# The passage between two steps of a graph layer on one core: the order of the last tiles' work

## The chip, the core and the metric

The kernel runs on one core of a Trainium2 chip. A core has five engines that run at the same time, each with a queue of its own in strict order: TensorE (PE in the profile; its weight loads are PEld), VectorE (DVE), ScalarE (ACT), GpSimd (POOL) and SyncE (SP), which here only issues DMAs. They wait for one another through semaphores. TensorE writes to PSUM; VectorE and ScalarE read it from there.

The metric is the device time of one execution in microseconds (us), lower is better. Several executions are timed; one more is profiled, and its trace gives the times of single instructions, counted from the start of the span.

## What is computed

A graph layer over N = 3327 nodes with D = 256 features, in two steps. `x` is normalised and passed through relu before (X below). Each step builds an attention matrix from the present features, keeps in each row only the largest probabilities that together reach 0.9, and multiplies; beside it the features are spread over a given sparse graph S.

```python
def _top_p_attention(X, W1, W2, W3):
    logits = (X @ W1.T @ W2.T) @ (X @ W3.T).T / TAU
    probs = softmax(logits)
    ...
    A = probs * mask          # mask: the largest that together reach TOP_P = 0.9
    return A / A.sum(-1)

R = S + I;  R = R / R.sum(-1)
Xf = Xa = X;  Z = 0
for n in range(2):
    A = _top_p_attention(Xa, W1, W2, W3)
    Xf = R @ Xf
    Xa = A @ Xa
    Z = Z + Xf @ U1[n].T + Xa @ U2[n].T
out = x + layernorm(X + Z) * ln_g + ln_b
```

## The kernel before

**Tiles and stages.** The 3327 rows are 26 tiles of 128 (NT = 26). For each step and tile these stages run:

- `weights`: the logits of a tile against all keys, in four chunks (CUT = 4). Each chunk is two matmuls into the PSUM buffer `pl` (L597) and an exponential by ScalarE into the row buffer `e` (L601, the last chunk L607 and L609). A chunk n needs the keys of its quarter of the tiles; the fourth needs the last tile's keys.
- `measured`: guesses the threshold of each row from sums over `e`. In step 1 (`measured_twice`) ScalarE passes three times over the whole row (`through`, L632), with small instructions of ScalarE, VectorE and POOL between the passes (L684, L685, L698 to L713). It needs the law of the tile (`ms`): from `law_once` for the first three tiles of step 1, from `laws` (eight groups of up to three tiles, L555 to L562) for the others.
- `settle`: VectorE finds the exact threshold: a pass over `e` (L728), maxima of segments (L733, L740), and the pass that sets the small entries to zero (L759 in two parts for the first and the last tile, L762 otherwise).
- `Sums`: TensorE transposes `e` in seven blocks of four (`turn`, L808), ScalarE copies them out (L810), TensorE multiplies with the features (`sum`, L822) into the single PSUM buffer `pa`. At the end of a tile of step 0 ScalarE scales the sum into `xa` (L831).
- `spread` (graph sum): six products of gathered neighbours into the single PSUM buffer `pr` (L928), then VectorE's reciprocal and sum (L1123, L1124), and in step 0 a store to `vx` in device memory. The neighbours of step 1 are gathered by POOL from `vx` (L920, indirect DMAs) and so need all of `vx`.
- `first_end` (step 0): the scaled sum is transposed (L477, copied at L480), multiplied with both U2 at once into `pr` (512 columns, L947), and the results are copied by ScalarE to `xw` (the features that step 1 sums) and, with `x0` added by POOL, to the store `sx`. Then `prep` makes the tile's keys and queries (L488, copied at L496 and L497), and for the tiles in COUNTED their part of the Gram matrix `gsum`.
- `moments` (L510 to L515) turns `gsum` into the matrix from which `law_once` (L528, L530, L536 to L543) and `laws` take mean and variance. `prove` checks the thresholds with some thirteen small VectorE instructions.

**The order.** All stages are Python generators. The loop over `i` from -1 to NT + 1 in each step has seven parts per round (PARTS = 7), and for each part a string names which generators take a step: `s` spread, `e` first_end, `w` logits, `m` and `n` measured, `d` and `c` settle, `l` laws, `g` gathers, and so on. After a part's letters follow the transposes and the sum of one block, tile i - 1 in step 0. The strings stand in BEGIN (first rounds of step 0), PLAN, OPEN (first rounds of step 1) and LAST. At the end of the function a dependency is added from each instruction of TensorE, ScalarE, VectorE and POOL to the next one in the text, so these queues run in the order of the text; SP's queue is tied that way only up to the start of step 1.

**Around the passage.** In step 0, round i = 25 sums tile 24, round 26 sums tile 25 but for its last block, and round 27 does that block. Each of the rounds also runs `spread` and `first_end` of tile i - 2. Three chunks of logits of tiles 0, 1 and 2 of step 1 (`begun`) run in rounds 24, 25 and 26. At the end of round 26 stand `moments` and three `law_once`. Step 1 begins with the last chunk of tile 0's logits, `prove(0)` and two memsets; its round -1 measures tile 0 with the laws' groups between, round 0 settles tile 0 and measures tile 1, and in round 1 the first sum starts.

The lines that order this before:

```python
for c in ("lcnwqsepb" if i > -1 else "cnwqsepb") if step else "ocmwqseph" + "b" * (i > 0):
    run(work[c])
if step == 0 and i == NT:
    moments(1, gsum)
    for t in range(3):
        live[1, t]["ms"] = returned(law_once(1, t))
```

Of the kernel before, what the change touches and what calls it, by code (L numbers as in the profile page):

```python
# [9 lines left out]
F32 = mybir.dt.float32  # L10
# [4 lines left out]
ALU = mybir.AluOpType  # L15
# [321 lines left out]
DIRECT = 4  # L337
LIST = 16
KT = DIRECT + 2
BEHIND = mybir.DependencyInfo(mybir.DependencyClass.Sync, mybir.DependencyReason.DATA)  # L340
IN_ORDER = mybir.DependencyInfo(mybir.DependencyClass.NoSync, mybir.DependencyReason.DATA)
NONE = NP - 1
# [3 lines left out]
def guess_graph_layer(ctx, tc, x, adj, w1t, w2t, w3t, u1t, u2t, ln_g, ln_b, out, flag):  # L346
# [122 lines left out]
        G.tensor_tensor(rstd, rstd, half[:, :1], ALU.pow)  # L469
        return rstd  # L470

    def transposed(rows, pt=None, xT=None):

        if pt is None:
            pt = ps_t.tile([P, 4, P], F32, tag="pt", name="pt")
        for c in range(ND):
            PE.transpose(pt[:, c, :], rows[:, c * P : (c + 1) * P], ident)  # L477
        if xT is None:
            xT = tpool.tile([P, ND, P], F32, tag="xT", name="xT", bufs=2)
        S.copy(xT, pt[:, :ND, :])  # L480
        return xT


    def prep(xT, t):
        j, h = divmod(t, 2)
        pk = ps_t.tile([P, 4, P], F32, tag="pt", name="pk")
        for c in range(ND):
            PE.matmul(pk[:, 0, :], wk[:, c, h * DA : h * DA + P], xT[:, c, :], start=c == 0, stop=c == ND - 1)  # L488
        if t in COUNTED:
            for c in range(ND):  # L490
                PE.matmul(pk[:, 1, :DA], xT[:, c, :], wk[:, c, :DA], start=c == 0, stop=c == ND - 1)
        kp = (low, high)[h]
        kr = krs[:, t // 2 % 2, :]
        if t in COUNTED:
            S.copy(kr[:, :DA], pk[:, 1, :DA])
        S.copy(after[kp, j, :], pk[kp, 0, :])  # L496
        S.copy(query_of(t), pk[query_at(t), 0, :])  # L497
        if t not in COUNTED:
            return
        yield  # L500
        pg = ps_t.tile([P, 4, P], F32, tag="pt", name="pg")
        PE.matmul(pg[:DA, 0, : DA + 1], kr[:, :DA], kr, start=True, stop=True)
        gt = small.tile([DA, DA + 1], F32, tag="gt", name="gt", bufs=2)
        S.copy(gt, pg[:DA, 0, : DA + 1])
        G.tensor_tensor(gsum, gsum, gt, ALU.add)
# [15 lines left out]
            nc.sync.dma_start(qT[rows], query_of(t))  # L521
        return qT

    def law_once(step, t):

        pq = ps_t.tile([P, 4, P], F32, tag="pt", name="pq")
        pm = pq[:, 1:3, :].rearrange("p a b -> p (a b)")[:, : 2 * DA + 2]
        PE.matmul(pm, query_of(t), qm[query_at(t), step, :], start=True, stop=True)  # L528
        mq = small.tile([P, 2 * DA + 2], F32, tag="mq", name="mq", bufs=2)
        S.copy(mq, pm)  # L530
        yield


        ms = small.tile([P, 9], F32, tag="ms", name="ms")
        col = lambda k: ms[:, k : k + 1]
        V.scalar_tensor_tensor(mq[:, : DA + 1], mq[:, : DA + 1], 1.0, mq[:, DA + 1 :], ALU.mult, ALU.mult,  # L536
                               accum_out=col(1))
        minus = mq[:, 2 * DA + 1 :]
        G.tensor_tensor(col(2), col(1), half[:, 1:2], ALU.pow)
        G.tensor_scalar(ms[:, 3:7], of_s[:, step, :], col(2), 1.0e-4, ALU.mult, ALU.add)  # L540
        G.tensor_scalar(col(7), col(1), 0.5, minus, ALU.mult, ALU.subtract)
        G.tensor_scalar(col(7), col(7), 0.25, LNY[step] - 0.25 * math.log(0.1 / N), ALU.mult, ALU.add)
        G.tensor_scalar(col(8), col(1), minus, col(4), ALU.subtract, ALU.add)  # L543
        return col


    def laws(ts):

        at = lambda k, a, b: law[:, k, a:b]
        few_of = [ts[h::2][n : n + 3] for n in range(0, len(ts), 3) for h in range(2)]  # L550
        for few in filter(len, few_of):
            pq = ps_t.tile([P, 4, P], F32, tag="pt", name="pq")
            pm = pq.rearrange("p a b -> p (a b)")[:, : 3 * (2 * DA + 2)].rearrange("p (t n) -> p t n", t=3)
            for k, t in enumerate(few):
                PE.matmul(pm[:, k, :], query_of(t), qm[query_at(t), 1, :], start=True, stop=True)  # L555
            wide = scan.tile([P, NP], F32, tag="w", name="wide")
            mq = wide[:, : 3 * (2 * DA + 2)].rearrange("p (t n) -> p t n", t=3)
            V.tensor_copy(mq[:, : len(few)], pm[:, : len(few)])
            V.tensor_copy(law[:, 2, few[0] : few[-1] + 1 : 2], mq[:, : len(few), DA])
            for k, t in enumerate(few):  # L560
                V.scalar_tensor_tensor(mq[:, k, : DA + 1], mq[:, k, : DA + 1], 1.0, mq[:, k, DA + 1 :],
                                       ALU.mult, ALU.mult, accum_out=at(1, t, t + 1))  # L562
            yield
        a, b = ts[0], ts[-1] + 1
        s, var, m = (at(k, a, b) for k in range(3))
        S.activation(s, var, AF.Ln, bias=con(7))
        S.activation(s, s, AF.Exp, scale=0.5)
        for k, c in ((3, SQG[1][0]), (4, SQG[1][2]), (5, -SQK[1][0]), (6, -SQK[1][2])):
            G.tensor_scalar(at(k, a, b), s, c, 1.0e-4, ALU.mult, ALU.add)
        G.tensor_tensor(at(4, a, b), at(4, a, b), var, ALU.add)  # L570
        G.tensor_tensor(at(4, a, b), at(4, a, b), m, ALU.add)
        G.tensor_scalar(m, m, 0.25, LNY[1] - 0.25 * math.log(0.1 / N), ALU.mult, ALU.add)
        G.tensor_scalar(var, var, 0.125, None, ALU.mult)
        G.tensor_tensor(var, var, m, ALU.add)
# [361 lines left out]
    def stores():  # L936
        while kept:
            t, sv = kept.popitem()
            nc.sync.dma_start(sx[t], sv)

    def first_end(t):
        aT = transposed(live.pop(("r", t)))
        stores()
        yield
        pz = ps_r.tile([P, 2 * D], F32, tag="pr", name="pz")
        for c in range(ND):
            PE.matmul(pz, aT[:, c, :], u2[:, c].rearrange("p n d -> p (n d)"), start=c == 0, stop=c == ND - 1)  # L947
        S.copy(xw[:, t, :], pz[:, D:])
        sv = row.tile([P, D], F32, tag="sv", name="sv", bufs=2)
        S.copy(sv, pz[:, :D])  # L950
        G.tensor_tensor(sv, sv, x0[:, t, :], ALU.add)
        yield
        kept[t] = sv
        yield from prep(aT, t)
# [30 lines left out]
        V.tensor_copy(flag, pf[:1, 0, :1])  # L985

    none = iter(())
    own_of, kept = {}, {}
    live, ohs, acs, xgs, done, early = {}, {}, {}, {}, [], {}

    def run(work, n=99):
# [139 lines left out]
    def refetch(t):  # L1131
# [14 lines left out]
    BEGIN = {-1: ("mba", "mmbba", "mwwbbaa", "bmwwb", "", "", ""),  # L1146
             0: ("mdbb", "mcdbb", "medbwwbp", "mdbb", "gmpdbwwb", "hgdbgbq", "hgq"),
             1: ("ggmdsssbb", "gmcdgsssbb", "gedbwwbp", "bmsdg", "gmpdeg", "hgdwwqg", "hgemgqo"),
             2: ("gmdsssa", "gmcdsssga", "gedawwpg", "gmsdga", "gmspdea", "ohgdawwqg", "gehmgq")}
    OPEN = {-1: ("llcmss", "lnms", "lwwnfd", "lcmdsssggggg", "fmgdswqdf", "llmdf", "lmwfdm"),  # L1150
            0: ("cmssggg", "nms", "wwnfd", "cmdsss", "fdsmgwqdf", "mdf", "mwd"),
            1: ("cmss", "nms", "wwnfd", "cmdsssgggg", "fdsmwqdf", "mgdf", "mwdg")}
    OPEN[2] = OPEN[3] = OPEN[1]
    spacing = itertools.chain(spaced((0, 1)), *(spaced((t,)) for t in range(2, NT)))
    fetching = itertools.chain(*(refetch(t) for t in range(NT)))
    LATE = (1, 4)
    BLOCKS = ({}, {1: (0, 1), 2: ()})
    trace, begin = nc.cur_bb.bb.instructions, len(nc.cur_bb.bb.instructions)
    work = dict(m=none, d=none, f=none)
    later = {}  # L1160
    ordered = []
    for step in range(2):
        sums = Sums(step, live, xw if step else x0, AHEAD[step])

        for i in range(-1, NT + 2):
# [3 lines left out]
                ordered.append(len(trace))  # L1169
            if step == 1 and i == -1:  # L1170
                run(begun[0])
                prove(0)
                for e in es[4:]:
                    G.memset(e[:, N:NP], 0.0)
            work.update(
                n=work["m"],
                c=work["d"],
                d=settle(step, i, live[step, i]) if valid(i) else none,
                m=measured(step, live[step, i + 1]) if valid(i + 1) else none,
                s=spread(step, i - 2 + 2 * step) if valid(i - 2 + 2 * step) else none,  # L1180
                w=later.pop((step, i + 2), none),
                e=first_end(i - 2) if step == 0 and valid(i - 2) else none,
                a=itertools.islice(lister, 6) if step == 0 else none,
# [9 lines left out]
                next(later[step, i + 3])  # L1193
            if step == 0 and i >= NT - 2 and i < NT + 1:

                work["w"] = itertools.islice(begun[i - NT + 2], CUT - 1)
            if step == 0 and i >= NT - 3 and i < NT:
                next(begun[i - NT + 3])
            if i == -1:
# [1 line left out]
            if step == 0 and i == 0:  # L1201
                work["w"] = begun[2]
            for k in range(PARTS):
                g = PARTS * (i - 1) + k - LATE[step]
                summing = valid(g // PARTS)
                if step and valid((g + AHEAD[1]) // PARTS):
# [17 lines left out]
                run(work["m"])  # L1224
            if step == 0 and i == -1:
                G.memset(es[2][:, N:NP], 0.0)
            if step and i < 1:
                next(fetching)
            for c in ("lcnwqsepb" if i > -1 else "cnwqsepb") if step else "ocmwqseph" + "b" * (i > 0):
                run(work[c])  # L1230
            if step == 0 and i == NT + 1:
                stores()
            if step == 0 and i == NT:
                moments(1, gsum)
                for t in range(3):
                    live[1, t]["ms"] = returned(law_once(1, t))
    run(work["f"])

    for engine, since, until in ((PE.engine, begin, None), (S.engine, begin, None), (V.engine, begin, None),
# [48 lines left out]
```

## Time and profile before

| what | us |
|---|---|
| three timed runs, median (lowest to highest) | 1344.52 (1342.86 to 1345.33) |
| the profiled execution, its own time | 1346.05 |
| its span, first to last instruction | 1344.3 |
| TensorE busy in the span | 1259.3 (94%) |
| VectorE busy | 1151.8 (86%) |
| ScalarE busy | 1074.2 (80%) |
| GpSimd busy | 1017.4 (76%) |

The busy shares are means over the span. Step 0 runs to about 741 us, step 1 from there. In the windows from 200 to 690 us TensorE is busy for 99.9% of the time, and between 900 and 1300 us for 95 to 97%. Between 740 and 760 us it is busy for 13.49 of 20 us, and between 760 and 800 us for 24.54 of 40. A group in the trace is named by line, engine and tile: `pa` is the sum of weighted features, `pr` the graph sum, `pz` the U2 product, `pk` the keys, `pl` logits, `pt` transposes, `pq` moments and laws. Where a row has a bracket, it gives the idle time of the engine in front of it and what ended it.

### The profile page before, as it was taken

Reading aid. Unit: us, or ns where it says so; the run is one execution under the profiler, and the core shown is the slowest. Engines: PE = TensorE matmul, PEld = TensorE weight load, DVE = VectorE, ACT = ScalarE, POOL = GpSimd, SP = SyncE. Lnnn points to the kernel's source line nnn. Section 1 sums busy time; section 2 is a strip of 40 time slices with the busy share of each in tenths; the row PEclk is TensorE's granted clock in tenths of the full one; section 3 lists DMA queues with packets and bytes.
Section 4 is the critical chain, followed back from the end, with each engine's and each line's share of the span. In section 5 each row is a group of like instructions: output and inputs, shape, how many; then the busy total and the mean of one; then the engine's idle time right before and its main releaser. Section 6 shows DMA issues by size and latency. Waiting matters only on the chain.

```text
span 1344.3 us, 22106 instructions
## 1 busy us (share of the span) xinstructions
PE 1259.3 (94%) x6396; PEld 956.0 (71%) x6396; DVE 1151.8 (86%) x3481; ACT 1074.2 (80%) x2315; POOL 1017.4 (76%) x1411
## 2 busy tenths in 40 slices
PE   5989899999999999999999589999999999999985
PEld 4535677778777787777777367777777777777774
DVE  6876899999999999999981698888998898988993
ACT  5476798888878888888853889899998999999951
POOL 6214888888888888887883587888888888888852
PEclk9999999999999999999999789999999999999998
DMA  7744455454555555455433213132222223131200
GB/s 265 254 132 133 123 153 160 141 157 136 144 157 145 154 142 155 137 152 154 117 103 91 79 50 90 54 95 62 86 79 69 87 65 95 53 95 61 82 24 23
DMA packets 100723, 153.13 MB, mean 114 GB/s; under 512 B 16849, under 2 KB 67152, under 8 KB 100592
## 3 DMA queue, kind: packets, MB, share of 16 engines
q1 hardware_dynamic: 83056, 108.72, 25.5%
q0 software_dynamic: 16640, 42.69, 12.7%
q8 instruction: 53, 0.87, 0.3%
q14 instruction: 78, 0.64, 0.2%
q10 hardware_dynamic: 896, 0.21, 0.1%
HBM read 120.88 MB, written 27.28 MB: 110 GB/s over the span
## 4 chain that ended last, share of the span: by engine, by line
PE 52%; ACT 25%; POOL 10%; DVE 7%; issue 3%; DMA 0%; SPq 0%; DVEq 0%; POOLq 0%; ACTq 0%
PE pa L822 23%; ACT ja L632 14%; PE pl L597 7%; PE pt L808 6%; PE pr L928 5%; PE pz L947 3%; PE pz L1016 3%; POOL g L710 3%; ACT eT L810 3%; ACT e L601 2%; POOL xg L920 2%; DVE cand L733 1%; ACT x L601 1%; DVE bb L740 1%; POOL g L707 1%
## 5 line engine op out<-in xcount | busy, mean ns | idle before, releaser
L822 PE MATMUL pa<-xw,eT 128*128 128x256 f32 x1352 | 323.7, 384 | 4.0 <-DVE s L958 3.8
L632 ACT ACTIVATE ja<-e,g 128x3328 uint8<-128x3328 f32 x106 | 325.7, 3073 | 0.1
L822 PE MATMUL pa<-x,eT 128*128 128x256 f32 x1352 | 322.0, 379 | 0.0
L822 PEld LDWEIGHTS pa<-xw,eT 128*128 128x128 f32 x1352 | 250.7, 190 | 64.0 <-issue 20.9
L822 PEld LDWEIGHTS pa<-x,eT 128*128 128x128 f32 x1352 | 242.8, 190 | 25.5
L733 DVE MAX8 cand<-w 128x8 f32<-128x168 f32 (+1 forms) x1040 | 253.4, 317 | 0.0
L810 ACT COPY eT<-pt 128x512 f32<-128x512 f32 (+1 forms) x364 | 198.4, 553 | 45.4 <-PE pt L808 39.1
L899 POOL DMA_INDIRECT ac<-in_adj,index x130 | 188.2, 1448 | 60.1 <-issue 26.5
L920 POOL DMA_INDIRECT xg<-bx,index x130 | 184.4, 1419 | 48.6 <-issue 16.2
L808 PE MATMUL pt<-ident,e 128*128 128x128 f32 x1144 | 176.0, 276 | 17.1 <-DVE e L759 8.5
L920 POOL DMA_INDIRECT xg<-vx,index x130 | 164.3, 1264 | 34.0 <-issue 32.9
L808 PEld LDWEIGHTS pt<-ident,e 128*128 128x128 f32 x1144 | 138.8, 143 | 71.0 <-issue 44.1
L728 DVE SCALAR_TENSOR_TENSOR w<-e,g 128x3328 f32<-128x3328 f32 x44 | 164.4, 3737 | 9.1 <-ACT g L713 8.2
L928 PE MATMUL pr<-xg,ac 128*128 128x257 f32 (+1 forms) x520 | 141.5, 396 | 10.4 <-DVE s L1124 7.0
L762 DVE SCALAR_TENSOR_TENSOR e<-e,rec 128x3328 f32<-128x3328 f32 x40 | 147.2, 3680 | 0.6
L601 ACT ACTIVATE e<-pl 128x832 f32<-128x832 f32 x132 | 113.9, 865 | 27.7 <-PE pl L597 24.5
L928 PEld LDWEIGHTS pr<-xg,ac 128*128 128x128 f32 x520 | 93.8, 194 | 37.5 <-issue 14.6
L597 PE MATMUL pl<-both,qT 64*128 64x416 f32 x416 | 100.0, 545 | 7.7 <-ACT e L601 4.3
L597 PE MATMUL pl<-after,qT 64*128 64x416 f32 x416 | 95.9, 555 | 1.8 <-ACT e L601 1.4
L852 DVE TENSOR_REDUCE fm<-at 128x4 f32<-128x512 f32 (+1 forms) x133 | 84.3, 634 | 0.0
L740 DVE MAX8 bb<-cand 128x8 f32<-128x160 f32 x234 | 75.6, 323 | 4.6
L632 ACT ACTIVATE ja<-x,g 128x3328 uint8<-128x3328 f32 x24 | 73.7, 3069 | 0.0
(261 smaller groups left out, 2045.3 us busy)
## 6 DMA issues: line engine op xcount, KB each, us to landing
at<-in_adj SPq DMA_DIRECT2D x114, 256.0 KB
cx<-ac SPq DMA_DIRECT2D x26, 384.0 KB
ac<-cx SPq DMA_DIRECT2D x26, 384.0 KB
wide<-in_adj SPq DMA_DIRECT2D x8, 832.0 KB
e<-in_adj SPq DMA_DIRECT2D x6, 832.0 KB
own<-bx SPq DMA_DIRECT2D x26, 128.5 KB
x<-in_x SPq DMA_DIRECT2D x13, 256.0 KB
qT<-both SPq DMA_DIRECT2D x104, 32.0 KB
```

Source lines behind the costliest of these rows:

```text
L597: PE.matmul(pl[:, a, :wd], qT[p, :], keys_of(step, a).rearrange("p a b -> p (a b)")[:, c : c + wd], start=True, stop=True)
L601: S.activation(e.rearrange("p (a n) -> p a n", a=2)[:, :, c : c + wd], pl[:, :, :wd], AF.Exp, accum_out=za[:, n : n + 1])
L632: S.activation(ja, e, f, bias=guess, scale=sign, accum_out=total)
L728: V.scalar_tensor_tensor(w, e, col(16), e, ALU.is_lt, ALU.mult, accum_out=d2)
L733: V.max(cand[:, 8 * s : 8 * s + 8], w[:, s * SEG : min(NP, (s + 1) * SEG)])
L762: V.scalar_tensor_tensor(e, e, at(1), e, ALU.is_ge, ALU.mult, accum_out=ra)
L808: PE.transpose(pt[:, j, :], e[:, (j0 + j) * P : (j0 + j + 1) * P], ident)
L810: S.copy(eT[:, :w, :], pt[:, :w, :])
L822: PE.matmul(self.pa, eT[:, c - 4 * k, :], self.xa[:, j, :], start=c == 0, stop=c == NT - 1)
L899: G.indirect_dma_start(out=ac[:, k, :], out_offset=None, in_=rows, in_offset=bass.IndirectOffsetOnAxis(ap=index[:, t, k : k + 1], axis=0), ...
L920: G.indirect_dma_start(out=xg[:, k, :w], out_offset=None, in_=rows, in_offset=bass.IndirectOffsetOnAxis(ap=index[:, t, k : k + 1], axis=0))
L928: PE.matmul(pr[:, :w], ac[:, k, :], own if k == KT - 1 else xg[:, k, :w], start=k == 0, stop=k == KT - 1)
```

## The change

Tiles 23, 24 and 25 (ENDS = 3) have their U2 product taken out of `first_end`: there the sum is transposed and the keys are made at once, and the transposed sum is kept in `ends`. The graph sums of tiles 24 and 25 are taken out of rounds 26 and 27. Both come back in a new generator `middle`, whose letter is `x`, in round -1 of step 1: two graph sums, the laws of tiles 1 and 2, then three `last_end`. In those, VectorE copies and adds in place of ScalarE and POOL. For tile 25 VectorE also does the copies of the transposed sum, the keys and the queries.

Moments, the law of tile 0 and `prove(0)` go into round 26, in front of parts 2, 4 and 5. Of tile 1's logits, one chunk stays in round 25, and two go to round 27, around the last tile's transposes. OPEN[-1] has a new order: the measuring of tile 0 begins one part earlier, the laws' groups stand later, the eighth in round 0, and the last logits of tile 1 and tile 2 come after the third pass and at the end. The seven gathers of round -1 remain seven, in another place. The memsets of step 1's `e` buffers 4 and 5 move to the end of round 0. In `laws` only the second half of each tile's columns is copied from PSUM; the other operand is read there.

```diff
+ENDS = 3
-    def transposed(rows, pt=None, xT=None):
+    def transposed(rows, pt=None, xT=None, copy=S.copy):
...
-    def prep(xT, t):
+    def prep(xT, t, copy=S.copy):
...
-        S.copy(after[kp, j, :], pk[kp, 0, :])
-        S.copy(query_of(t), pk[query_at(t), 0, :])
+        copy(after[kp, j, :], pk[kp, 0, :])
+        copy(query_of(t), pk[query_at(t), 0, :])
...
-            V.tensor_copy(mq[:, : len(few)], pm[:, : len(few)])
-            V.tensor_copy(law[:, 2, few[0] : few[-1] + 1 : 2], mq[:, : len(few), DA])
+            V.tensor_copy(mq[:, : len(few), DA + 1 :], pm[:, : len(few), DA + 1 :])
+            V.tensor_copy(law[:, 2, few[0] : few[-1] + 1 : 2], pm[:, : len(few), DA])
             for k, t in enumerate(few):
-                V.scalar_tensor_tensor(mq[:, k, : DA + 1], mq[:, k, : DA + 1], 1.0, mq[:, k, DA + 1 :],
+                V.scalar_tensor_tensor(mq[:, k, : DA + 1], pm[:, k, : DA + 1], 1.0, mq[:, k, DA + 1 :],
                                        ALU.mult, ALU.mult, accum_out=at(1, t, t + 1))
...
+    def last_end(t, aT):
+        pool, tag = ((ps_r, "pr"), (ps_a, "pa"))[t % 2]
+        pz = pool.tile([P, 2 * D], F32, tag=tag, name="pz")
+        for c in range(ND):
+            PE.matmul(pz, aT[:, c, :], u2[:, c].rearrange("p n d -> p (n d)"), start=c == 0, stop=c == ND - 1)
+        V.tensor_copy(xw[:, t, :], pz[:, D:])
+        sv = row.tile([P, D], F32, tag="sv", name="sv", bufs=2)
+        V.tensor_tensor(sv, pz[:, :D], x0[:, t, :], ALU.add)
+        nc.sync.dma_start(sx[t], sv)
+
     def first_end(t):
+        if t >= NT - ENDS:
+            last = t == NT - 1
+            aT = adjp.tile([P, AD, P], F32, tag="at", name="aT", bufs=2)[:, :ND, :] if last else None
+            aT = transposed(live.pop(("r", t)), xT=aT, copy=V.tensor_copy if last else S.copy)
+            ends.append((t, aT))
+            stores()
+            yield
+            yield from prep(aT, t, V.tensor_copy if last else S.copy)
+            return
...
+             NT + 1: ("", "weweee", "", "", "", "", ""),
...
-    OPEN = {-1: ("llcmss", "lnms", "lwwnfd", "lcmdsssggggg", "fmgdswqdf", "llmdf", "lmwfdm"),
-            0: ("cmssggg", "nms", "wwnfd", "cmdsss", "fdsmgwqdf", "mdf", "mwd"),
+    OPEN = {-1: ("mxx", "mxl", "mxlggg", "mgxl", "mwxl", "ml", "lmlggg"),
+            0: ("cmssggg", "lnms", "wwnfd", "cmdsss", "fdsmgwqdf", "mdf", "mwd"),
...
+    def middle():
+
+        for t in (NT - 2, NT - 1):
+            run(spread(0, t))
+            yield
+        both_ = [law_once(1, t, V.tensor_copy) for t in (1, 2)]
+        for made_ in both_:
+            next(made_)
+        for t, made_ in zip((1, 2), both_):
+            live[1, t]["ms"] = returned(made_)
+        yield
+        for t, aT in ends:
+            last_end(t, aT)
+            yield
...
             if step == 1 and i == -1:
                 run(begun[0])
-                prove(0)
-                for e in es[4:]:
-                    G.memset(e[:, N:NP], 0.0)
+                work["x"] = middle()
...
-                s=spread(step, i - 2 + 2 * step) if valid(i - 2 + 2 * step) else none,
+                s=spread(step, i - 2 + 2 * step) if valid(i - 2 + 2 * step) and (step or i < NT) else none,
...
-                work["w"] = itertools.islice(begun[i - NT + 2], CUT - 1)
+                work["w"] = itertools.islice(begun[i - NT + 2], 1 if i == NT - 1 else CUT - 1)
+            if step == 0 and i == NT + 1:
+                work["w"] = itertools.islice(begun[1], 2)
...
             for k in range(PARTS):
+                if step == 0 and i == NT and k == 2:
+                    moments(1, gsum)
+                if step == 0 and i == NT and k == 4:
+                    work["y"] = law_once(1, 0)
+                    next(work["y"])
+                if step == 0 and i == NT and k == 5:
+                    live[1, 0]["ms"] = returned(work["y"])
+                    prove(0)
...
-            if step and i < 1:
+            if step and i == 0:
                 next(fetching)
+            if step == 1 and i == 0:
+                for e in es[4:]:
+                    G.memset(e[:, N:NP], 0.0)
...
-            if step == 0 and i == NT:
-                moments(1, gsum)
-                for t in range(3):
-                    live[1, t]["ms"] = returned(law_once(1, t))
```

More of the change, by code (lines that the diff above doesn't have):

```diff
@@ L479, in transposed @@
             xT = tpool.tile([P, ND, P], F32, tag="xT", name="xT", bufs=2)
-        S.copy(xT, pt[:, :ND, :])
+        copy(xT, pt[:, :ND, :])
         return xT
-    def prep(xT, t):
+    def prep(xT, t, copy=S.copy):
         j, h = divmod(t, 2)
@@ L522, in asked, with law_once @@
         return qT
-    def law_once(step, t):
+    def law_once(step, t, copy=S.copy):
         pq = ps_t.tile([P, 4, P], F32, tag="pt", name="pq")
@@ L529, in law_once @@
         mq = small.tile([P, 2 * DA + 2], F32, tag="mq", name="mq", bufs=2)
-        S.copy(mq, pm)
+        copy(mq, pm)
         yield
@@ L987, in guess_graph_layer @@
     none = iter(())
-    own_of, kept = {}, {}
+    own_of, kept, ends = {}, {}, []
     live, ohs, acs, xgs, done, early = {}, {}, {}, {}, [], {}
```

## The prediction

> **What bounds the kernel now.** I first read the table of 20 us windows around the passage from step 0 to step 1, then the chain of waits through it, then the engines' timelines.
>
> ```profile
> core 0: us, PE busy (x) PEld busy (x) DVE busy (x) ACT busy (x) POOL busy (x), PEclk, DMA share, GB/s
> ...
> 700.00:720.00 20.00, 20.00 (x106) 15.63 (x105) 1.97 (x9) 8.13 (x20) 10.62 (x13) 1.00 0.45 134
> 720.00:740.00 20.00, 18.49 (x87) 13.43 (x85) 3.92 (x25) 5.21 (x15) 5.72 (x16) 1.00 0.14 42
> ```
>
> From 700 to 731 us TensorE is busy without a gap while VectorE works 2 to 4 us in 20: the last sums of step 0 are bound by TensorE alone. The chain of waits says the same, and then what follows (start, net length, engine, tile, line):
>
> ```profile
> 709.65 1.30 PE pr L928 x6
> 710.95 0.44 PE pt L808 x4
> 711.39 0.87 PE pa L822 x4
> 712.25 1.30 PE pr L928 x6
> ...
> 722.01 1.72 PE pz L947 x4
> ...
> 725.90 0.90 PE pl L597 x4
> ...
> 728.89 0.45 PE pk L488 x4
> 729.34 1.73 PE pa L822 x8
> 731.07 0.38 PE pq L512 x2
> ...
> 734.77 0.86 PE pa L822 x4
> ...
> 737.81 1.96 PE pz L947 x4
> 739.76 0.44 PE pk L488 x4
> 740.21 1.00 PE pl L597 x3
> 741.78 0.95 ACT e L607 x2
> 744.47 0.39 ACT g L624
> 745.22 3.05 ACT ja L632 x2
> 748.28 0.84 ACT e L607 x2
> 749.26 0.84 ACT e L607 x2
> ...
> 754.80 3.17 ACT ja L632 x2
> ```
>
> Between the end of the sixth of tile 25's seven blocks (729.34 + 1.73 = 731.07) and the exponential of step 1's last logits of tile 0 (741.78) lie 10.7 us: moments, laws, the graph sum, the last block, the U2 product, the key product. From there ScalarE's chain of measuring (three passes over e, L632, and two exponentials between them) runs to 761.1 (the wait in front of L728 below ends with it), and VectorE settles tile 0:
>
> ```profile
> 741.86 0.56 DVE L558 COPY wide<-pq 128x390 f32<-128x390 f32 x1 [0.59 <-PE pq L555]
> ...
> 743.29 0.56 DVE L558 COPY wide<-pq 128x390 f32<-128x390 f32 x1
> ...
> 761.12 3.68 DVE L728 SCALAR_TENSOR_TENSOR w<-e,g 128x3328 f32<-128x3328 f32 x1 [2.09 <-ACT g L713]
> ...
> 769.63 0.21 DVE L684 TENSOR_SCALAR g<-oa,g 128x1 f32<-128x1 f32 x1 [1.83 <-ACT ja L632]
> ...
> 779.02 0.08 DVE L759 DVE_READ_ACCUMULATOR e<-e,rec 128x1 f32 x1
> ```
>
> At 779.1 the first part of e is masked, and TensorE starts step 1's sums. From there step 1 is a loop of 26 like tiles, so I count a shift of that moment as a shift of the end.
>
> **The change, part by part.** *Last two rounds of step 0 (i = 25, 26).* Removed from TensorE: the U2 products of tiles 23 and 24 (2 x 1.72 = 3.44), the graph sum of tile 24 (2 x 1.30 = 2.60), two logit chunks of tile 1 (2 x 0.90 = 1.80). Added: moments (0.38) and one law (about as much, 0.37). One new wait: the 1.30 of graph sum at 712.25 covered ScalarE's copy of the finished sum out of the single pa buffer; now only the next block's transposes (0.44) stand there. I take 0.3; none and 1.3, the cover removed, are the ends. Sum: 3.44 + 2.60 + 1.80 - 0.75 - 0.3 = 6.8 us. VectorE's and ScalarE's windows above leave room, so nothing else is late: the sixth block ends at 724.3. The proof (thirteen small VectorE instructions) falls into VectorE's idle time beside the sum, and its cost is nothing there; without that cover it would be some 3 us.
>
> *Sixth block to last logits.* The order is now: last block 0.86, a chunk of tile 1's logits 0.90 (it hides ScalarE's scaling of the sum), two transposes (half of the 0.44 of four, with a wait 0.3), a second chunk 0.90 (it hides VectorE's copy of 256 columns; 390 take 0.56, so about 0.45), key product 0.45, VectorE's copy of the keys with its handover about 0.5, product to exponential about 0.6. Sum 4.5 against 10.7. The exponential starts at 728.8 instead of 741.8: **13.0 us gained here**.
>
> *The middle work, i = -1 of step 1.* Everything taken out comes back: two graph sums (5.2 us of TensorE), three U2 products (5.2 by the net row), two laws, with VectorE's work behind each, and three stores of s, two of vx, on SP. TensorE was mostly idle in this stretch, so its own time is covered. What counts is VectorE, whose queue is strictly in order; ahead of settling tile 0 now stand:
> - the two graph sums: TensorE 728.4 to 731.0, VectorE's reciprocal and sum 0.7, then the second (one pr buffer, so one after the other), VectorE done at about 735.2. What stands behind in VectorE's queue waits for this;
> - two law copies and products, about 1.15;
> - eight groups of laws. One takes 1.43 now (743.29 - 741.86). Half the columns are copied; at 0.56 for 390, 195 columns save about 0.2, so 1.23, and 9.9 for eight;
> - three last ends, two passes of 256 columns each, about 0.82: 2.45. No row shows them on VectorE; the smallest cost is 0.4 (two of 0.2 as L684), the largest 1.1 (two of the 0.56 of 390 columns); I take the middle because the width is known;
> - the small instructions of measuring, 1.4 (seven like L684).
>
> That is 14.9 us from 735.2, so 750.1; waits for the U2 products, which alternate with the groups on TensorE, cost about 1.4 (ends 0 and 3 x 1.72): 751.5. The eighth group stands on TensorE behind the first two products of tile 0's graph sum in step 1 and the last logits of tile 2, so 0.5 more if TensorE's clock is full and about 2.2 if it is halved. Settling starts between 752.0 and 753.7.
>
> The row that bears on this clock:
>
> ```profile
> 751.00:754.00 3.00, 0.00 (x0) 0.00 (x0) 0.56 (x3) 2.40 (x3) 1.43 (x2) 0.50 0.44 119
> ```
>
> The granted clock was 0.50 in a window in which TensorE had nothing. After the change TensorE has short groups every 1.2 us from 744.7 on. [...]
>
> *ScalarE and POOL as lower bounds.* ScalarE's chain took 761.1 - 741.8 = 19.3; one of the two exponentials between its passes (748.28 to 750.25, about 1.0 each) goes behind the chain and the other into a wait, so 17.7 alone: 746.5. VectorE's queue holds L684 back by about 1.7 and L698 by about 0.9, so the guess of tile 0 comes at about 749.5, before VectorE is free. POOL carries two law chains and then seven gathers:
>
> ```profile
> 746.60 1.10 POOL L920 DMA_INDIRECT xg<-vx,index  x1 [0.15 <-issue]
> ```
>
> The first gather, at 746.60 now, needs the vx store of tile 25 (SP, at about 735.3) and POOL's laws, so about 740.3; at 1.25 each with the gap, three are issued by 744 and TensorE wants the first two at about 750. That hides them.
>
> *From settling to the first transposes.* Now 779.1 - 761.1 = 18.0, of which 1.83 is the wait of L684. ScalarE goes on to tile 1 after the guess (749.5), one exponential of tile 2 (1.1) and the 8.6 of guess and two passes (769.6 - 761.0), so L684 of tile 1 is ready at 759.2; VectorE gets there 6.7 after its start, 758.7 to 760.4. From L684 to 779.1 are 9.5 us. The first part of e is ready at 768.7 to 769.9; middle 769.3, against 779.1: **9.8 us gained.**
>
> *Laws read from PSUM.* The products of L561 now take an operand from PSUM. [...] No row shows that instruction with PSUM.
>
> The profiled execution took 1346.05 us, 1.75 above its span of 1344.3; less 9.8 it would be 1336.25. The median of the three runs is 1344.52; less 9.8 it is **1334.7**.
>
> **The rivals.**
> 1. *VectorE's queue is shorter than I count, and ScalarE's chain sets the start.* Guess at 746.5, L684 of tile 1 at 756.2, first part of e at 765.7: gain 13.4, time 1331.1. For it: VectorE sat idle in front of L728 before (2.09). Against: its queue has some 5 us more now and starts late. 15%.
> 2. *VectorE's queue is longer.* The waits between U2 products and groups reach their upper end (+3.8), and the last ends theirs (+0.8): settling at 757, gain about 5.5, time 1339. The half clock and the three products in single buffers speak for it. 22%.
> 3. *The change does not do what it says:* in rounds 25 and 26 another engine takes TensorE's place, and the middle work pays the rest back. Time 1344.5. Against: VectorE 1.97, ScalarE 8.13 of 20. 5%.
> 4. *Slower:* the eighth group, and VectorE's settling behind it, wait on TensorE for tile 0's first gathers, these for the vx stores, which SP may place behind other transfers. From a first landing at 759 (9 us after TensorE wants it) nothing is left, and every later us is lost; at 762, with the stores behind all six query loads, 1347.5. Against: the store is ready 11 us earlier than the gather started before. 5%.
>
> The forecast itself keeps 50%, with 1333 to 1336.5 as its own range; 3% go to a different rhythm of step 1, whose loop I did not follow.
>
> **How the numbers follow.** The range 1331 to 1341 takes in the forecast, the first rival and most of the second (its upper end is a gain of 3.5); outside lie some 17%. 0.2% (2.7 us) is about what a measurement tells from no change. Faster: 50 + 15 + 22 and one of the 3 open: 0.88. Same: the third rival and one, 0.06. Slower: the fourth and one, 0.06.
>
> **What would show it.** Right: the sixth block of tile 25 ends about 7 us earlier (else the first part is wrong); the last exponential of tile 0 starts near 729; in front of L728 of tile 0 VectorE is busy or waits for TensorE's pq, not for ScalarE's L713 (else rival 1); the first gather starts near 740 (else rival 4); step 1's first transposes come near 769, and from there to the end the time is as before, 565 us (else step 1's loop changed).

## The result and the profile after

| | before | after |
|---|---|---|
| median of 19 runs each (lowest to highest), us | 1345.86 (1342.63 to 1350.3) | 1341.05 (1336.88 to 1344.52) |
| the profiled execution, its span | 1344.3 | 1335.7 |
| last exponential of tile 0's logits starts | 741.78 | 730.13 |
| settling of tile 0 starts | 761.12 | 756.68 |
| first transposes of step 1 start | 779.25 | 772.91 |

The ratio of the times is 0.9961 [0.9949, 0.9973]: some 5.2 us faster (3.6 to 6.9), where 9.8 were forecast. Of the 6.35 us between the forecast time, 1334.7, and the measured one, 1.34 are the starting point: the kernel before has a median of 1345.86 in these runs, and the forecast went out from 1344.52. The first mark comes 11.7 us earlier, the second only 4.4: more than half of the lead is lost between the last logits and the settling of tile 0. Lines behind L337 have moved by one (before's L728 is L729 here, L607 is L608), and those behind the new `last_end` by twenty (L1124 is L1144). L946, L947 and L949 are now the product, the copy and the addition of `last_end`.

The windows of the changed kernel (columns as in the prediction), first 20 us and then finer:

```profile
720.00:740.00 20.00, 18.62 (x84) 12.21 (x82) 5.20 (x29) 13.06 (x25) 2.94 (x10) 1.00 0.23 69
740.00:760.00 20.00, 17.96 (x69) 11.47 (x68) 12.84 (x67) 14.96 (x28) 15.26 (x28) 0.76 0.32 93
...
738.00:748.00 10.00, 10.00 (x46) 5.35 (x45) 5.23 (x32) 7.18 (x11) 8.22 (x18) 1.00 0.54 160
748.00:751.00 3.00, 1.45 (x13) 1.10 (x12) 2.69 (x22) 1.63 (x7) 1.36 (x6) 0.91 0.33 92
751.00:754.00 3.00, 2.98 (x9) 2.52 (x10) 1.81 (x16) 2.12 (x9) 2.37 (x5) 0.50 0.10 26
```

Between 740 and 760 us TensorE, busy for 13.49 of 20 us before, is now busy for 17.96. From 738 to 748 it has no gap at all, while VectorE works 5.23 of those 10 us. The engine that the prediction called covered is the full one.

The chain of waits of the changed kernel (start, net length, engine, tile, line) through the same stretch:

```profile
721.61 4.32 PE pa L823 x20
725.93 0.90 PE pl L598 x4
726.83 0.37 PE pt L478 x2
727.20 0.90 PE pl L598 x4
728.10 0.64 PE pk L489 x4
728.74 1.35 PE pl L598 x4
730.09 2.82 PE pr L929 x12
...
737.54 0.93 PE pq L556 x6
738.48 1.91 PE pz L946 x4
740.39 0.86 PE pq L556 x6
741.26 1.91 PE pz L946 x4
743.17 0.75 PE pq L556 x5
743.92 1.51 PE pl L598 x8
745.43 1.93 PE pz L946 x4
```

The first six rows are the new end of step 0 with the last logits of tile 0, and the seventh is the graph sum of tile 24. The first row holds the last three blocks without a break and ends at 725.93 (721.61 + 4.32); the last block is four of its twenty matmuls, 0.86 us, so the sixth ends at 725.07. It was 731.07. From 737.54 to 747.36 the chain stays on TensorE: the groups of laws (pq), the U2 products (pz) and the last logits of tiles 1 and 2 (pl) add up to 9.80 of 9.82 us. VectorE's timeline shows the other side, the bracket being its idle time in front of the row and what ended it:

```profile
737.21 0.48 DVE L531 COPY mq<-pq 128x130 f32<-128x130 f32 x2
...
738.52 0.36 DVE L559 COPY wide<-pq 128x195 f32<-128x195 f32 x1 [0.54 <-PE pq L556]
...
740.43 0.42 DVE L947 COPY xw<-pz 128x256 f32<-128x256 f32 x1 [0.99 <-PE pz L946]
740.77 0.41 DVE L949 TENSOR_TENSOR sv<-pz,x 128x256 f32<-128x256 f32 x1
...
743.21 0.42 DVE L947 COPY xw<-pz 128x256 f32<-128x256 f32 x1 [0.62 <-issue]
...
747.38 0.42 DVE L947 COPY xw<-pz 128x256 f32<-128x256 f32 x1 [2.39 <-PE pz L946]
...
752.69 0.36 DVE L559 COPY wide<-pq 128x195 f32<-128x195 f32 x1 [0.79 <-PE pq L556]
...
755.85 0.29 DVE L559 COPY wide<-pq 128x130 f32<-128x130 f32 x1 [2.25 <-issue]
...
756.68 3.69 DVE L729 SCALAR_TENSOR_TENSOR w<-e,g 128x3328 f32<-128x3328 f32 x1
...
763.27 0.21 DVE L685 TENSOR_SCALAR g<-oa,g 128x1 f32<-128x1 f32 x1
```

Of the 19.47 us from the copies of the two laws to the settling, VectorE waits 7.58: 0.99, 0.62 and 2.39 for the three U2 products, 0.54 and 0.79 for groups, 2.25 for the eighth group. The prediction had 1.9 to 3.6. Its own work is 11.89, where the prediction had 14.9. Two brackets say "issue" instead of an engine. In the trace of the same kernel taken once more (run e1_again) both have a name:

```profile
742.35 0.42 DVE L947 COPY xw<-pz 128x256 f32<-128x256 f32 x1 [0.62 <-PE pz L946]
...
754.63 0.29 DVE L559 COPY wide<-pq 128x130 f32<-128x130 f32 x1 [2.25 <-PE pq L556]
```

### The profile page after: what moved, and what is told of

The parts are those of the page before. It is cut to its first block, busy times and chain, and to the rows that moved or that the text cites. A ratio compares the mean times of both kernels' runs of the same rounds, so it can differ in the third digit from the quotient of the medians.

```text
span 1335.7 us, 22104 instructions
## 1 busy us (share of the span) xinstructions
PE 1260.7 (94%) x6396; PEld 954.8 (71%) x6396; DVE 1151.9 (86%) x3492; ACT 1070.7 (80%) x2304; POOL 1005.5 (75%) x1408
## 4 chain that ended last, share of the span: by engine, by line
PE 51%; ACT 17%; POOL 16%; DVE 10%; issue 4%; DMA 0%; POOLq 0%; DVEq 0%; SPq 0%; ACTq 0%
PE pa L823 22%; ACT ja L633 9%; PE pl L598 7%; PE pt L809 6%; PE pr L929 5%; POOL xg L921 4%; PE pz L967 3%; PE pz L1036 3%; DVE cand L734 2%; ACT eT L811 2%; POOL g L711 2%; ACT e L602 2%; POOL g L712 2%; POOL g L676 1%; DVE w L729 1%
## 5 line engine op out<-in xcount | busy, mean ns | idle before, releaser
L900 POOL DMA_INDIRECT ac<-in_adj,index x130 | 184.0, 1416 | 58.4 <-issue 26.8
L921 POOL DMA_INDIRECT xg<-bx,index x130 | 187.2, 1440 | 48.5 <-issue 14.8
L921 POOL DMA_INDIRECT xg<-vx,index x130 | 149.2, 1148 | 34.1 <-issue 29.9
L729 DVE SCALAR_TENSOR_TENSOR w<-e,g 128x3328 f32<-128x3328 f32 x44 | 164.8, 3746 | 6.3 <-ACT g L714 5.3
L763 DVE SCALAR_TENSOR_TENSOR e<-e,rec 128x3328 f32<-128x3328 f32 x40 | 147.2, 3681 | 0.6
```

The costliest lines, as they stand in the source:

```text
L729: V.scalar_tensor_tensor(w, e, col(16), e, ALU.is_lt, ALU.mult, accum_out=d2)
L763: V.scalar_tensor_tensor(e, e, at(1), e, ALU.is_ge, ALU.mult, accum_out=ra)
L900: G.indirect_dma_start(out=ac[:, k, :], out_offset=None, in_=rows, in_offset=bass.IndirectOffsetOnAxis(ap=index[:, t, k : k + 1], axis=0), ...
L921: G.indirect_dma_start(out=xg[:, k, :w], out_offset=None, in_=rows, in_offset=bass.IndirectOffsetOnAxis(ap=index[:, t, k : k + 1], axis=0))
```

## The experiments

The single traces differ by up to 5.5 us at some 105 us into the span (the same settling starts between 104.53 and 110.05) and by little more behind that, so in the table below the marks are counted from one event of step 0: VectorE's settling of tile 24, at 661.16 in the trace before and 660.63 in the one after. Each number is the start of a row of that run's timelines, less that event's start.

| trace | last exponential of tile 0 | settling of tile 0 | first transposes | settling of tile 1 to that of tile 25 | end of the span |
|---|---|---|---|---|---|
| before | 80.62 | 99.96 | 118.09 | 515.84 | 683.14 |
| b1_before | 80.64 | 99.96 | 118.11 | 514.24 | 681.62 |
| after | 69.50 | 96.05 | 112.28 | 513.16 | 675.07 |
| e1_again | 68.77 | 94.96 | 111.21 | 513.99 | 674.80 |
| e2_group8 | 68.76 | 92.96 | 109.19 | 514.69 | 673.52 |
| e3_one_end | 72.20 | 96.46 | 112.71 | 515.06 | 677.37 |
| e4_u2_first | 68.77 | 95.33 | 111.55 | 514.37 | 675.64 |
| e7_old_laws | 68.76 | 95.12 | 111.34 | 514.12 | 675.10 |
| e5_behind | 68.76 | 89.79 | 107.65 | 515.28 | 672.59 |
| e6_packed | 68.77 | 87.07 | 107.21 | 513.54 | 670.38 |

At the first three marks two traces of one kernel agree to 0.02 us (before, b1_before) or 1.1 (after, e1_again; in the first trace after, VectorE settled tile 25 late and TensorE waited for it at 701 us). In the expectations, theory A is that VectorE's queue waits for TensorE, which now carries the three U2 products and the eighth group behind the first products of tile 0's graph sum. Theory B is its rival, in each expectation as it is stated there: something other than TensorE holds the same place. (In the expectations of e1_again and b1_before the two theories are about the spread between traces.) The times do not tell the changed kernel, e2, e3, e4 and e7 apart: their intervals of the ratio overlap. What is read from these runs is read from one trace of each.

**e1_again and b1_before.** The changed kernel and the kernel before, unaltered.

> The changed kernel, unaltered, for a second trace. In its first trace settling of tile 0 started at 756.68 us (before: 761.12) and the first transposes of step 1 at 772.91 (before: 779.25), a lead of 6.3 us, which then grew to 9.0 by the last tile. Theory A (the passage itself gives about 6 us, and step 1's loop adds or takes a few us by chance): settling again within 0.5 us of 756.7, the lead at the last tile anywhere from 4 to 9, ratio 0.996. Theory B (the passage itself varies from run to run): settling more than 1 us away from 756.7.

> The kernel before, unaltered, for a second trace. Counted from the start of settling tile 24 in step 0 (so that the first 660 us, which differ by up to 6 us between traces, fall out), its first trace has settling of tile 0 in step 1 at 99.96 us, the first transposes of step 1 at 118.09 and the end at 683.14; four traces with the change have the transposes at 109.2 to 112.7 and the end at 673.5 to 677.4. Theory A (the lead at the passage is kept to the end): transposes at 118 again, end at 681 to 684. Theory B (the first trace of before had an unlucky step 1, and the change's step 1 gives part of the lead back): transposes at 118, end below 680.

Measured: 1339.83 us against 1344.83, ratio 0.9964 [0.9952, 0.9977]; the kernel before 1346.11 in one run. The lead at the marks is 11.9 us, 5.0 us and 6.9 us (118.11 - 111.21, with 80.64 - 68.77 and 99.96 - 94.96 for the first two). For b1_before this is theory A: transposes at 118.11, end at 681.62. For e1_again it is theory B by its mark, since settling started at 755.46, more than 1 us from 756.68. From the common event the difference is 1.09 us: 0.73 stand already at the last exponential, and 0.36 are the wait for the seventh group, 0.43 us here and 0.79 in the first trace. The column between two settlings shows no lead given back in step 1's loop: 514.2 and 515.8 before, 513.2 and 514.0 after.

**e2_group8.** The eighth group goes back in front of tile 0's graph sum.

```diff
-    OPEN = {-1: (..., "ml", "lmlggg"),
-            0: ("cmssggg", "lnms", ...
+    OPEN = {-1: (..., "ml", "lmllggg"),
+            0: ("cmssggg", "nms", ...
```

> The eighth group of laws goes back ahead of the first products of tile 0's graph sum in TensorE's order. Theory A (VectorE's queue, in order, waits for TensorE in the middle work; 2.25 us of it in front of group eight): settling of tile 0 starts at 754.7 (2.0 earlier than 756.68), the first transposes near 771, the time 1.5 to 2 us shorter. Theory B (ScalarE's and POOL's chain of measuring sets the start): settling stays at 756.7, time the same.

Measured: 1338.9 us, ratio 0.9954 [0.9941, 0.9967]; settling and first transposes 2.0 us earlier than in e1_again. VectorE's last wait is gone:

```profile
757.59 0.36 DVE L559 COPY wide<-pq 128x195 f32<-128x195 f32 x1 [0.59 <-PE pq L556]
...
759.44 3.68 DVE L729 SCALAR_TENSOR_TENSOR w<-e,g 128x3328 f32<-128x3328 f32 x1
```

The row of L729 has no bracket: behind the last group VectorE waited for nothing else. As A has it, the 2.25 us were TensorE's; that the time gets 1.5 to 2 us shorter, as A also says, the medians do not show (0.9, within the intervals). (Its trace starts some 6 us late, so the absolute times are higher.)

**e3_one_end.** Only tile 25's U2 product is moved; those of tiles 23 and 24 stay in step 0, as before the change, and their copies and additions stay with ScalarE and GpSimd.

```diff
-ENDS = 3
+ENDS = 1
```

> Only tile 25's U2 product goes behind its keys; those of tiles 23 and 24 stay in rounds 25 and 26, where each costs TensorE 1.72 us. Theory A (the middle work fills TensorE, and a U2 product costs there about what it saved): the last exponential of tile 0 comes 3.4 us later (733.6 against 730.13), but settling starts between 754 and 757, so the time is the same or up to 2 us shorter. Theory B (the prediction's view: TensorE's time in the middle is covered): settling 3 to 3.4 us later, near 760, time 3 us longer.

Measured: 1339.75 us, ratio 0.9961 [0.9948, 0.9974]. The last exponential comes 3.43 us later, twice a product's 1.72; settling and first transposes only 1.5 us later. So a product taken out of step 0 buys 1.7 there and costs, together with VectorE's two passes behind it, about 1 in the middle: between the two theories. Two of the three waits for products are gone, and one row shows what stood behind them:

```profile
749.70 0.27 DVE L699 TENSOR_SCALAR g<-oa,g 128x1 f32<-128x1 f32 x1 [2.29 <-ACT ja L633]
```

With fewer products VectorE waits 2.29 us for ScalarE's passes, which follow the later exponential.

**e4_u2_first.** The last U2 product goes in front of the last logits of tiles 1 and 2.

```diff
-    OPEN = {-1: (..., "mgxl", "mwxl", "ml", "lmlggg"),
+    OPEN = {-1: (..., "mgxl", "mxwl", "ml", "lmlggg"),
```

> Tile 25's U2 product goes ahead of the last logits of tile 1 in TensorE's order. Theory A (VectorE's longest wait in the middle, 2.39 us for that product, is on the path): settling starts 1.5 us earlier, near 755.1. Theory B (what it waits for next, POOL's gathers in front of POOL's part of the measuring, takes its place): settling stays within 0.5 us of 756.7.

Measured: 1338.92 us, ratio 0.9965 [0.9952, 0.9978]; settling 0.37 us later. This is the number of theory B, but not for its reason:

```profile
744.79 0.42 DVE L947 COPY xw<-pz 128x256 f32<-128x256 f32 x1 [0.99 <-PE pz L946]
...
747.05 0.36 DVE L559 COPY wide<-pq 128x195 f32<-128x195 f32 x1 [1.51 <-PE pq L556]
```

The wait for the third product falls from 2.39 to 0.99, and the next group's rises from nothing to 1.51. Whichever stands first, VectorE needs both, and TensorE's sum over the stretch is the same. The 0.37 us themselves say nothing of the order: the seventh group's wait is 0.80 here and 0.43 in e1_again, the same difference as between the two traces of the changed kernel. I had taken the row with the longest bracket for the cause; the cause is the length of TensorE's queue.

**e7_old_laws.** The copy of all 390 columns and the products from SBUF come back in `laws`; all else is as after the change.

```diff
-            V.tensor_copy(mq[:, : len(few), DA + 1 :], pm[:, : len(few), DA + 1 :])
+            V.tensor_copy(mq[:, : len(few)], pm[:, : len(few)])
```

> The changed kernel with the laws' groups as before (all columns copied from PSUM, the products read SBUF), about 0.45 us more of VectorE for each of eight groups. Theory A (TensorE paces the middle, and VectorE waits for it): settling of tile 0 0.3 to 1.5 us later than 94.96 after settling tile 24, because most of the 3.6 us falls into VectorE's waits. Theory B (VectorE's own work paces it): 3 to 3.6 us later.

Measured: 1338.52 us, ratio 0.9954 [0.9935, 0.9973]; settling 0.16 us later, though VectorE has some 0.4 us more to do in each of eight groups (738.85 to 740.18 for the first, against 738.52 to 739.44 after the change).

```profile
740.77 0.42 DVE L947 COPY xw<-pz 128x256 f32<-128x256 f32 x1 [0.58 <-PE pz L946]
...
743.54 0.42 DVE L947 COPY xw<-pz 128x256 f32<-128x256 f32 x1 [0.20 <-PE pz L946]
...
747.72 0.42 DVE L947 COPY xw<-pz 128x256 f32<-128x256 f32 x1 [1.93 <-PE pz L946]
...
755.65 0.43 DVE L559 COPY wide<-pq 128x260 f32<-128x260 f32 x1 [0.76 <-PE pq L556]
```

The three waits for products shrink from 0.99, 0.62 and 2.39 to 0.58, 0.20 and 1.93, about 0.4 each, and the eighth group's falls from 2.25 to 0.76: the added work sits inside the waits. This is less than even theory A expected. So the part of the change that shortens `laws` is worth nothing measurable here, and VectorE's own work, which the prediction summed with most care, is not what set the start of settling. One reserve: with the products read from SBUF, TensorE's seventh group waits only for VectorE's copy (L559), where in e1_again it waits for the products (L562); it starts 89.61 us behind the common event against 89.66. So behind the last U2 product a part of the added work may be made up by the buffer that comes free earlier.

**e5_behind.** The three U2 products go behind tile 0's graph sum of step 1, where TensorE waited for the first transposes; the eighth group stands as in e2. TensorE adds `x0` through the identity, and ScalarE copies the results at the start of round 1, so VectorE's two passes behind each product are gone from the middle as well.

```diff
+    def ends_later():
+        pl, pa = ps_l.tile(...), ps_a.tile(...)
+        pzs = (pl[:, 0, :], pl[:, 1, :], pa)
+        for (t, aT), pz in zip(ends, pzs):
+            PE.matmul(pz, aT[:, 0, :], ..., start=True, stop=False)
+            PE.matmul(pz[:, :D], ident, x0[:, t, :], start=False, stop=False)
+            PE.matmul(pz, aT[:, 1, :], ..., start=False, stop=True)
+        yield
...
-    OPEN = {-1: ("mxx", "mxl", "mxlggg", "mgxl", "mwxl", "ml", "lmlggg"),
-            0: ("cmssggg", "lnms", "wwnfd", "cmdsss", ...
-            1: ("cmss", ...
+    OPEN = {-1: ("mxx", "mxl", "mlggg", "mgl", "mwl", "ml", "lmllggg"),
+            0: ("cmssggg", "nms", "wwnfd", "cmdsssz", ...
+            1: ("czmss", ...
```

> Group eight as in the run before it, and the three U2 products behind tile 0's graph sum of step 1, in TensorE's idle time while tile 0 settles; x0 is added by TensorE, the copies are ScalarE's at the start of round 1. Counted from settling tile 24. Theory A (TensorE's added work in the middle holds VectorE's queue back, the U2 products above all): settling at 89 to 90 (94.96 with the change alone, 92.96 with group eight moved), the transposes at 107.5 (111.2, 109.2), the time 3 to 4 us below the changed kernel. Theory B (ScalarE's chain and POOL's gathers are already the bound): settling at 92 or later, transposes at 109, the time as with group eight moved.

Measured: 1335.03 us against 1344.55 before, ratio 0.9925 [0.9895, 0.9955]. As theory A has it, settling comes 5.2 us earlier than in e1_again, 3.2 of them beyond e2: that is what the products and VectorE's passes behind them cost in the middle. The two are not separated: from the copies of the two laws to the settling VectorE's own work is 2.5 us shorter than in e2, and its waits only fall from 5.12 to 4.46, since the three waits for products go and others come. The first transposes come 3.6 us earlier than in e1_again; two other waits are next:

```profile
744.42 0.27 DVE L699 TENSOR_SCALAR g<-oa,g 128x1 f32<-128x1 f32 x1 [2.58 <-POOL g L689]
...
749.60 3.68 DVE L729 SCALAR_TENSOR_TENSOR w<-e,g 128x3328 f32<-128x3328 f32 x1
...
757.82 0.21 DVE L685 TENSOR_SCALAR g<-oa,g 128x1 f32<-128x1 f32 x1 [1.54 <-ACT ja L633]
```

The row named L699 waits for GpSimd, which issues its gathers ahead of the small instructions of measuring; L685 of tile 1 waits for ScalarE's passes.

**e6_packed.** As e5, with all groups moved forward, GpSimd's gathers behind the first small instructions, and the last logits of tile 2 apart from those of tile 1 (a new letter, `v`).

```diff
-    OPEN = {-1: ("mxx", "mxl", "mlggg", "mgl", "mwl", "ml", "lmllggg"),
+    OPEN = {-1: ("mxx", "mxl", "ml", "wmggll", "mvll", "m", "lmlggggg"),
```

> As the run before, and the gathers go behind POOL's part of the measuring (two in its middle, five after it), the laws' groups into VectorE's waits for ScalarE's passes, and the last logits of tiles 1 and 2 apart, one in front of the third pass and one behind it. Theory A: with TensorE's work out of the way POOL's gathers and ScalarE's chain bound the middle, and the new order shortens that: settling at 87, transposes at 105, the time 5 to 6 us below the changed kernel. Theory B (the gathers, now later, hold tile 0's graph sum and with it VectorE's sum inside settling): settling at 87, but transposes at 107 or later.

Measured: 1335.2 us, ratio 0.9925 [0.9898, 0.9953], the same as e5. Settling is 2.7 us earlier, the first transposes only 0.4. Three rows of three engines, from GpSimd's, TensorE's and VectorE's timelines:

```profile
748.39 3.42 POOL L921 DMA_INDIRECT xg<-vx,index  x1 [0.30 <-issue]
...
753.92 2.59 PE L929 MATMUL pr<-xg,ac 128*128 128x256 f32 x4 [2.62 <-DMA xg<-vx,index]
...
757.40 0.48 DVE L1144 SCALAR_TENSOR_TENSOR s<-pr,rrs,s 128x256 f32<-128x256 f32 x1 [3.82 <-PE pr L929]
```

This is theory B: VectorE waits 3.82 us for tile 0's graph sum, and that for the late gathers. VectorE's queue now comes to this sum before its transfers are through: the mechanism of the prediction's rival 4, with a small price.

## Why the prediction was wrong

**The step that failed** is the sentence on the middle work, "TensorE was mostly idle in this stretch, so its own time is covered. What counts is VectorE". With it went the term for the waits for the U2 products, 1.4 us, and the lack of any term for the waits for the groups ahead of the eighth. Measured, the three products cost VectorE 4.00 us of waiting and two groups another 1.33. Between 740 and 760 us TensorE was busy for 13.49 of 20 us even before the change, which is not mostly idle, and the change brings two graph sums and three products into the middle work, over ten microseconds. I worked out VectorE's queue instruction by instruction, and TensorE's not at all; then I set the waits for the products near the low end of their bounds, 0 and 5.2, without a row that favoured that end.

The forecast's late end for the settling was 735.2 + 14.9 + 1.4 + 2.2 = 753.7: start of the queue, VectorE's own work, waits for products, eighth group. Measured, it is 737.21 + 11.89 + 4.00 + 1.33 + 2.25 = 756.68. So the waits for products and groups are 3.9 us more than forecast and the start 2.0 later, and VectorE's own work is 3.0 less. The eighth group came out at the forecast's late end.

That the waits for the products are TensorE's is shown by the rows: TensorE has no gap from 738 to 748 us while VectorE waits. The two groups' waits are hand-overs both ways, since TensorE itself waited 0.56 and 0.80 us for VectorE in front of those groups. e2 takes the eighth group's wait out by moving that group alone. e4 shows that another order within TensorE's queue only moves a wait, and e7 that some 3 us more work on VectorE move the settling by 0.16. What the products alone cost is not shown, because e3 and e5 take VectorE's passes out together with them.

This was the second rival, at 22%: settling at 757, gain 5.5, time 1339. The run had 756.68, a gain of 5.2 by the ratio, and 1341.05, just above the upper end of the range. Its mechanism held in the waits, 5.33 us against its 5.2. Its other half did not: the last ends took the 0.82 of the forecast, 0.42 and 0.41. That its 757 comes so near is partly luck, since the start, 2.0 us later, and VectorE's own work, 3.0 less, are not in the rival and work against each other.

The other steps:
- *Removed in rounds 25 and 26, 6.8 us; last logits 13.0 us earlier.* Near: counted from the common event, the last logits come 11.1 us earlier in the trace after and 11.9 in e1_again, the sixth block 5.5 and 6.2. The order of the rows is as forecast; from the sixth block to the exponential it took about 5.1 (730.13 less the 725.07 that the chain gives) instead of 4.5.
- *Start of the queue.* The second graph sum was over at 737.2 instead of 735.2: TensorE began the first at 730.02, not at 728.4, and each took some 2.9 us (730.02 to 732.90, 733.72 to 736.57) instead of 2.6.
- *VectorE's own work, 14.9 us.* It was 11.89. A group takes about 0.92 (738.52 to the end of its last row at 739.44) instead of 1.23: the row behind the copy starts 0.27 us after it (738.52 to 738.79), where before it was 0.60 (741.86 to 742.46); it now reads PSUM and not the copy, and in e7, where it reads the copy again, the 0.60 are back (738.85 to 739.45). This error worked the other way and hid part of the first.
- *Settling to first transposes, 16.5 us by the forecast's middle values.* Right: 772.91 - 756.68 = 16.23, and the wait of 1.83 in front of L684 (now L685) is gone: the last row of VectorE's timeline above has no bracket.
- *Products that read PSUM.* The prediction had no row for them. In the fence below L562, with one operand from PSUM, takes 0.22 us, as L561 did before with both from SBUF.
- *The loop of step 1 keeps the lead.* Right, by the column between two settlings in the table.
- *The clock.* The prediction sets the 0.50 of the row of 751 to 754 beside TensorE's having nothing in that window. The row lies wholly behind the moment at which the clock fell, about 750.3, and TensorE's pause was only 1.1 us old at that moment (see the last section).
- *Rivals 1, 3 and 4.* ScalarE's chain did not set the start; TensorE did give up its time in step 0; the first gather started at 742.02, not late enough to matter here.

The first of these two rows is from the kernel before, the second from the one after:

```profile
742.81 0.22 DVE L561 SCALAR_TENSOR_TENSOR wide<-wide 128x65 f32<-128x65 f32 x1
```

```profile
739.07 0.22 DVE L562 SCALAR_TENSOR_TENSOR wide<-pq,wide 128x65 f32<-128x65 f32 x1
```

One thing stays open. The first transposes come 5.8 to 6.9 us earlier in the traces, and the end of the span, counted from the common event, 6.6 to 8.3, where the medians differ by 4.8 to 5.2. The intervals reach from 3.1 to 6.9, and the runs of either kernel spread over some 7.7 us; no run was made to settle the last microsecond or two.

## What to carry to other kernels

When work is moved into a gap, add up the queue of every engine that it uses in the gap, the one that looked idle first: two strict queues that hand single buffers to each other can wait at many of the hand-overs, here at six in 19.47 us. A wait names the instruction that came last, not the cause; swap the two things it could be, and if the wait only moves, the cause is the sum. Work moved off a bound stretch is worth more when it goes where that engine truly waits (here behind the graph sum, in front of the first transposes) than to the next place in the text; in the traces that was worth 1.5 us at the first transposes (e5 against e2), while the intervals of the two times overlap.

## What the runs showed of the hardware

**The clock halved without a long pause.** After the change TensorE was busy without a gap from 738 to 748.5 us, then in groups with gaps of 0.77 and 0.80 us, and in the second gap the granted clock fell to 0.50. Three windows (columns as in the prediction):

```profile
747.00:750.50 3.50, 2.45 (x19) 1.81 (x18) 2.90 (x19) 2.44 (x11) 1.82 (x4) 0.99 0.37 100
750.25:750.50 0.25, 0.00 (x0) 0.00 (x0) 0.25 (x5) 0.25 (x2) 0.21 (x1) 0.91 0.00 0
750.50:751.00 0.50, 0.00 (x0) 0.02 (x1) 0.40 (x7) 0.19 (x1) 0.44 (x2) 0.50 0.00 0
```

Two rows of TensorE's timeline, two like groups of six matmuls:

```profile
749.31 0.91 PE L556 MATMUL pq<-qm,both 64*128 64x130 f32 x6 [0.77 <-DVE wide L562]
751.01 1.64 PE L556 MATMUL pq<-qm,both 64*128 64x130 f32 x6 [0.80 <-DVE wide L562]
```

The prediction kept the half clock as its late end, and the eighth group's wait of 2.25 us is near the 2.2 of that end. In the 3.50 us up to the fall TensorE was busy for 2.45. In the kernel before, the clock fell at about 750.3 (0.62 on the mean from 750.25 to 750.50), only 1.1 us after TensorE's last group had ended at 749.17. In e5_behind TensorE paused for 3.45 us, from 742.90 to 746.35, and the mean clock from 736 to 750 was 0.88. With a single fall from 1.00 to 0.50 that puts the fall at about 746.6 (an estimate: 3.4 of the 14 us at half), some 0.3 us after that pause had ended. What decides on the fall stays open.

**An indirect DMA's issue took three times as long beside one VectorE pass.** After the change 342 of the 390 indirect DMAs in the trace occupy GpSimd for 0.94 to 1.26 us each; the gather at 748.39 in e6_packed took 3.42, and one at 758.03 after the change 3.16. Both ran beside VectorE's L729 (3.69 us), and both ended 0.8 us behind the end of that pass (751.81 against 750.98, 761.19 against 760.37). An issue at 756.71 after the change, which began 0.03 us behind the start of the pass, took only 1.01. The other 48 of the 390 took 2.24 to 4.56 us: each began 0.12 us or more behind the start of one of VectorE's passes over a row (L729, L760, L763) and ended 0.80 to 0.99 behind its end. Why these take so long is not shown.

**The start varies.** The settling of tile 24 in step 0 began between 659.81 and 662.68 us in nine of the ten traces and at 666.48 in the tenth, e2_group8, whatever the kernel; behind that point the first three marks of the table repeat to 0.02 us (before) or 1.1 (after).
